# The fourth block of exponentials of each pair of heads is added by an adding DMA instead of by VectorE, in layer 0's attention

## The chip, the core and the metric

The kernel runs on one core of one Trainium2 chip. The metric is the device time of one execution in microseconds. Several runs are made of a kernel, and the median is given. One further execution is taken with the hardware profiler. The page and the trace describe that one execution, and its own time stands beside its span (the time from its first instruction to its last).

The engines are named as in the profile: PE is TensorE's matrix multiplication and PEld its loading of weights, DVE is VectorE, ACT is ScalarE, POOL is GpSimd, SP is SyncE, which here only issues DMAs. L1212 is line 1212 of the kernel.

## What is computed

The reference is a stack of four transformer-like layers on x of shape (4, 512, 128) in float32. Each layer is half a feed-forward block, an attention, and half a feed-forward block again. The change touches layer 0's attention alone:

```python
x = x + 0.5 * _L0_ffn_ref(_layernorm(x, axis=-1), ...)     # 8 experts, the 2 best of each token
x = x + _L0_attn_ref(_layernorm(x, axis=-1), ...)          # here
x = x + 0.5 * _L0_ffn_ref(_layernorm(x, axis=-1), ...)
...
# _L0_attn_ref: 16 heads of 64 channels, low-rank q, k and v, rotary positions on q and k
scores = jnp.einsum('bhqd,bhkd->bhqk', q, k) * scale       # 512 x 512 for each image and head
attn = jax.nn.softmax(scores, axis=-1)
out = jnp.einsum('bhqk,bhkd->bhqd', attn, v)
out = out.transpose(0, 2, 1, 3).reshape(b, s, H * DH)
out = out @ w_out.T + residual
```

There are 4 images (the first axis of x) of 512 tokens each. The softmax needs, for each image, head and query, the sum of 512 exponentials over the keys. How this sum is formed is what changes.

## The kernel before

**Layer 0's attention** is `l0_attn_quick` (L1191 to L1309). It works through 32 pairs of heads in order: 4 images, 8 pairs in each. P is 128, the number of partitions, S is 512, the number of tokens of an image, and NT is 4, the blocks of 128 keys.

For one pair, the scores are computed transposed, with keys on the partitions and queries along the row. For each block t of 128 keys, `score` (L1199) multiplies the block's keys with all 512 queries, for both heads, into one `big` tile of PSUM, 128 x 1024 (L1203). ScalarE takes the exponential of it into `pT` (L1204). A `pT` tile holds two blocks, so it is 128 x 2 heads x 2 blocks x 512 queries, and a pair fills two of them, one for each half. The pool has three `pT` buffers (`bufs=3`, in the loop) and three `big` ones (L282).

Then `value` (L1214) multiplies the four blocks with V, adding up in PSUM (L1217), and `add_up` (L1206) adds the four blocks of exponentials elementwise, into the pair's slice of the tile `sums`. It adds the first two blocks to each other (L1209) and then the third and the fourth to the sum (L1212, twice). The sum over the 128 partitions is left for later. A tile `sums` has 8 slices of 512, so it serves 4 pairs, and an image uses two of them; the pool has two. A slice of `sums` that a pair writes lies in one piece of 1024 elements in each partition.

Each pair also prepares later pairs. `l0_project` (L1149) multiplies out q and k of the pair after the next (L1153), ScalarE copies them out of PSUM (L1155), and two DMAs from SP's queue swap even and odd partitions into `other` (L1158). `l0_turned` (L1161) then rotates q and k of the next pair with three operations of VectorE, L1164 twice and L1165.

**The end of an image** (`end`, L1219) runs during the first pairs of the next image. Sixteen matrix multiplications L1223 add `sums` over the partitions, picking each head's row, in the order k outer and c inner; the second tile of `sums` is read in the second eight, and a pair's two slices are those of one c. VectorE takes the reciprocal (L1229, into `rsum`), TensorE spreads it over the channels (L1237, into `big` tiles), VectorE scales U with it (L1239), and TensorE multiplies with the output weights (L1246), which VectorE adds to x (L353). For the last image there is no next pair, so these steps stand alone.

**Other work runs in between**, in small steps from generators. One is the layer norm of the next image (`l0_begin`, L1168, with L318 to L331, L1172 on GpSimd and hT L1176). One is the routing of tokens to experts for the second feed-forward block (`route`, L499 to L596): its scatters L586 are indirect DMAs from GpSimd, 8 for each image. One is the gathering of rows from the first feed-forward block (`back`, L831, L842 on GpSimd and L837 on VectorE). GpSimd also sets `comb` to zero (L551) and takes a power in each layer norm (L322).

**The order of the work.** In this stage TensorE's instructions stand in the order of the program (`manual_schedule` with PE alone). The order on the other engines is made when the program is built, by a scheduler with estimates of durations, so taking an instruction away or putting one in can move others. Each engine's queue runs strictly in its order. Semaphores are put in by the framework: a buffer is written again only when every reader of its last content is done. For the rest of the program, after this attention, the order is made by a planner in the kernel (`run`, with `clock`), whose costs do not depend on this stage.

Of the kernel before, what the change touches and what calls it, by code (L numbers as in the profile page):

```python
# [13 lines left out]
ALU = mybir.AluOpType  # L14
# [256 lines left out]
def program(ctx: ExitStack, tc: tile.TileContext, a: dict, out: bass.AP, worst):  # L271

    nc = tc.nc
# [917 lines left out]
    def l0_attn_quick(w, work, head, made, first, early, late):  # L1191
# [14 lines left out]
        def add_up(half, s, pT):  # L1206

            if half == 0:
                nc.vector.tensor_tensor(s, pT[:, :, 0, :], pT[:, :, 1, :], ALU.add)  # L1209
            else:  # L1210
                for m in range(2):
                    nc.vector.tensor_tensor(s, s, pT[:, :, m, :], ALU.add)  # L1212

        def value(t, po, V, pT):  # L1214
            for u in range(2):
# [50 lines left out]
        for n, (b, hp) in enumerate(todo):  # L1266
# [23 lines left out]
            for half in range(2):  # L1290
                for t in (2 * half, 2 * half + 1):
                    value(t, po, made[b][1], pTs[half])
                add_up(half, sums[hp // 4][:, 2 * (hp % 4) : 2 * (hp % 4) + 2, :], pTs[half])
# [1534 lines left out]
```

## Time and profile before

| what | value |
|---|---|
| median of 3 runs (lowest to highest) | 1305.28 us (1298.9 to 1309.57) |
| the profiled execution, its time | 1288.94 us |
| the profiled execution, its span | 1287.2 us |
| mean granted clock of TensorE, of full speed | 0.965 |
| layer 0's attention, from the first exponential to the last sum over partitions | about 212 to 550 us |
| L1212 in the stage: number, mean, busy | 64, 1220 ns, 78.1 us |
| L1209 in the stage: number, mean, busy | 32, 1221 ns, 39.1 us |

The table of the profile's page has one row for each engine: busy time, its share of the span, and how many instructions it ran. "Busy" for PE does not mean that it works at its best rate, since the ends of its instructions are modelled. In a timeline a row has the start in us, the duration in us, the engine, the line, the operation, the tile written and the tiles read, their shapes, and how many instructions were merged into the row. In square brackets stands how long the engine had been idle before it and what ended that. In a list of waits a row has the waiting engine with its tile and line, the engine waited for with its own, and then the total in us, how often, and the longest.

### The profile page before, as it was taken

To read this page: it belongs to the slowest core of one execution; us is meant where nothing else is said; L and a number is where in the kernel's file an instruction comes from. 1 tells how busy PE (TensorE), PEld (TensorE's weight loads), DVE (VectorE), ACT (ScalarE), POOL (GpSimd) and SP (SyncE) were. 2 spreads that over 40 slices of the span, in tenths; PEclk is the share of its full clock that TensorE was granted. 3 is DMA by queue.
4 is the path that set the end of the run, shared out by engine and by line. 5 is a ranking of instruction groups with operands and counts; after the bars stand their busy time and mean duration, and the time that the engine had idled before them with its cause. 6 is when DMAs were issued, how large, how long until landed. Compare 5 with 4: busy or idle time off the path is not lost.

```text
span 1287.2 us, 20162 instructions
## 1 busy us (share of the span) xinstructions
PE 1174.3 (91%) x6954; PEld 630.3 (49%) x6954; DVE 895.4 (70%) x2328; ACT 700.6 (54%) x1015; POOL 328.1 (25%) x320
## 2 busy tenths in 40 slices
PE   5899989999999999988899949989999999999995
PEld 3455644334335335355455548765596544543333
DVE  5597767888988988769667945868735873365233
ACT  2435535653644544533345523556757777787872
POOL 4340223032220400202123554533224121041000
PEclk9899989999999999989899987899999999999998
DMA  8123311121110210201321140000011000000000
GB/s 308 33 73 90 89 60 52 66 76 38 57 66 33 80 48 37 67 1 40 106 73 44 36 133 23 26 12 23 26 50 38 5 18 18 17 25 1 9 9 11
DMA packets 63490, 65.00 MB, mean 50 GB/s; under 512 B 11538, under 2 KB 53908, under 8 KB 62868
## 3 DMA queue, kind: packets, MB, share of 16 engines
q1 hardware_dynamic: 57236, 51.04, 11.9%
q0 software_dynamic: 6144, 12.60, 3.3%
q8 instruction: 58, 0.95, 0.3%
q14 instruction: 52, 0.42, 0.1%
HBM read 29.13 MB, written 17.69 MB: 36 GB/s over the span
## 4 chain that ended last, share of the span: by engine, by line
PE 63%; DVE 21%; issue 5%; DMA 3%; ACT 3%; POOL 2%; SPq 1%; DVEq 0%; POOLq 0%; ACTq 0%
PE big L1956 8%; PE one L1998 8%; PE big L1203 5%; PE one L1217 5%; PE big L761 4%; PE one L1541 3%; PE big L883 3%; PE one L1246 2%; PE big L606 2%; DVE sums L1212 2%; PE big L1153 2%; PE one L2475 1%; PE one L2019 1%; PE big L635 1%; PE one L794 1%
## 5 line engine op out<-in xcount | busy, mean ns | idle before, releaser
L1972 ACT ACTIVATE pT<-big 128x1024 f32<-128x1024 f32 (+1 forms) x224 | 205.0, 963 | 52.7 <-PE big L1956 44.3
L1204 ACT ACTIVATE pT<-big 128x1024 f32<-128x1024 f32 x128 | 125.7, 1034 | 55.7 <-PE big L1203 53.0
L1203 PE MATMUL big<-qk 64*128 64x512 f32 x512 | 127.5, 609 | 6.8 <-DVE U L1239 6.8
L1956 PE MATMUL big<-qkq,qkk 32*128 32x512 f32 (+3 forms) x1024 | 130.9, 555 | 0.1
L1217 PE MATMUL one<-pT,V 128*64 128x512 f32 x512 | 116.9, 598 | 0.0
L1998 PE MATMUL one<-pT,V 128*32 128x512 f32 (+3 forms) x1024 | 111.5, 522 | 2.5 <-DVE through L2029 0.8
L1504 POOL TENSOR_TENSOR rs<-rs,root 128x4 f32<-128x4 f32 x35 | 37.1, 1059 | 226.8 <-DVE rs L1502 183.5
L586 POOL DMA_INDIRECT sorted_x<-xn,irows x64 | 70.9, 1108 | 69.8 <-DVE share L558 22.4
L1212 DVE TENSOR_TENSOR sums<-sums,pT 128x1024 f32<-128x1024 f32 x64 | 78.1, 1220 | 5.7 <-ACT pT L1204 1.1
L1203 PEld LDWEIGHTS big<-qk 64*128 64x128 f32 x512 | 46.6, 187 | 69.5 <-issue 40.9
L1956 PEld LDWEIGHTS big<-qkq,qkk 32*128 32x128 f32 x1024 | 49.2, 184 | 61.8 <-issue 40.8
L883 PE MATMUL big<-w_w,xsT 128*128 x156 | 76.2, 620 | 2.5 <-ACT xsT L1355 2.4
L761 PE MATMUL big<-w_w,xsT 128*128 x156 | 73.5, 595 | 0.4 <-issue 0.4
L1217 PEld LDWEIGHTS one<-pT,V 128*64 128x64 f32 x512 | 33.9, 136 | 77.1 <-issue 72.4
L842 POOL DMA_INDIRECT yg<-sorted_y,ito x32 | 40.1, 1254 | 123.0 <-DMA sorted_y<-ys 61.8
L1294 ACT COPY U<-one 128x512 f32<-128x512 f32 x32 | 18.8, 587 | 94.7 <-PE one L1217 92.6
L606 PE MATMUL big<-xnT,w_w 128*128 128x512 f32 x128 | 61.4, 616 | 6.9 <-DVE u L611 5.8
L353 DVE TENSOR_TENSOR x<-x,one 128x512 f32<-128x512 f32 x31 | 21.2, 684 | 57.2 <-PE one L1541 33.1
L1984 DVE TENSOR_TENSOR pT<-pT,w_c_tri 128x256 f32<-128x256 f32 (+1 forms) x96 | 52.4, 563 | 2.5 <-ACT pT L1972 2.2
L608 ACT ACTIVATE t<-big,w_bs 128x512 f32<-128x512 f32 x32 | 21.7, 685 | 56.5 <-PE big L606 30.9
L322 POOL TENSOR_TENSOR rs<-rs,root 128x4 f32<-128x4 f32 x16 | 20.7, 1298 | 118.7 <-DVE rs L321 118.6
L1998 PEld LDWEIGHTS one<-pT,V 128*32 128x32 f32 x1024 | 23.9, 108 | 54.6 <-issue 37.9
(448 smaller groups left out, 2418.4 us busy)
## 6 DMA issues: line engine op xcount, KB each, us to landing
other<-qk SPq DMA_DIRECT2D x64, 256.0 KB, 2.2
xs<-sorted_x SPq DMA_DIRECT2D x78, 64.0 KB, 1.8
sorted_y<-ys SPq DMA_DIRECT2D x38, 128.0 KB, 1.8
w_w<-in_w SPq DMA_DIRECT2D x2, 2048.0 KB
w_l_w<-in_l_w SPq DMA_DIRECT2D x8, 256.0 KB, 3.2
w_l_w<-in_l_w SPq DMA_DIRECT2D x1, 2048.0 KB, 8.4
X<-row_x SPq DMA_DIRECT2D x8, 256.0 KB, 3.5
row_y<-y SPq DMA_DIRECT2D x8, 256.0 KB, 2.3
```

Source lines behind the costliest of these rows:

```text
L586: apart(nc.gpsimd.indirect_dma_start(out=sorted_x[:, :], out_offset=bass.IndirectOffsetOnAxis(ap=irows[:, b, j, t : t + 1], axis=0), in_=x ...
L606: nc.tensor.matmul(pa[:, m, :], lhsT=w["w13"][:, NE, m, odd, c * P : (c + 1) * P], rhs=xTs[b], start=True, stop=True)
L761: nc.tensor.matmul(pa[:, k, :], lhsT=st[u]["xT"][:, k * P : (k + 1) * P], rhs=w["w13"][:, bass.ds(st[u]["e"][k], 1), m].rearrange("p o a b ...
L883: nc.tensor.matmul(pa[:, k, :], lhsT=xT[:, k * P : (k + 1) * P], rhs=w["w13"][:, bass.ds(e[k], 1), m].rearrange("p o a b -> p (o a b)"), s ...
L1203: nc.tensor.matmul(sT[:, u, :], lhsT=k[r, t * P : (t + 1) * P], rhs=q[r, :], start=True, stop=True)
L1204: nc.scalar.activation(pT[:, :, t % 2, :], sT, AF.Exp, scale=scale)
L1212: nc.vector.tensor_tensor(s, s, pT[:, :, m, :], ALU.add)
L1217: nc.tensor.matmul(po[r, :], lhsT=V[:, t, :], rhs=pT[:, u, t % 2, :], start=(t == 0), stop=(t == NT - 1), tile_position=(0, 64 * u))
L1956: nc.tensor.matmul(sT[j // 2][:, j % 2, c : c + n], lhsT=keys[k][r, t * P : (t + 1) * P], rhs=turns[k, g][r, S - n :], start=True, stop=True)
L1972: nc.scalar.activation(p[:, :, :n], sets[i][h][:, :, :n], AF.Exp, scale=scale)
L1984: nc.vector.tensor_tensor(d, d, w["c_tri"].unsqueeze(1).unsqueeze(1).to_broadcast([P, 2, len(parts), P]), ALU.min)
L1998: nc.tensor.matmul(po[32 * j : 32 * j + 32, S - n :], lhsT=V[k % 2][:, t, NJ * g + j, :], rhs=us[i][j // 2][:, j % 2, c : c + n], start=(t ...
```

## The change

In `add_up`, the third block is still added by VectorE (L1212). The fourth is no longer: a DMA issued from GpSimd reads the fourth block out of `pT`, and adds it to the slice of `sums` while it writes. It moves 128 partitions x 2 heads x 512 numbers, so 512 KB, for each of the 32 pairs. The DMA waits for the addition before it and for the fourth exponential; the sum over the partitions and the next writer of that `pT` buffer wait for the DMA.

```diff
@@ -1208,8 +1208,8 @@
             if half == 0:
                 nc.vector.tensor_tensor(s, pT[:, :, 0, :], pT[:, :, 1, :], ALU.add)
             else:
-                for m in range(2):
-                    nc.vector.tensor_tensor(s, s, pT[:, :, m, :], ALU.add)
+                nc.vector.tensor_tensor(s, s, pT[:, :, 0, :], ALU.add)
+                nc.gpsimd.dma_start(out=s, in_=pT[:, :, 1, :], accum_op=ALU.add)
 
         def value(t, po, V, pT):
             for u in range(2):
```

## The prediction

> **What bounds the kernel now.** I read first the page's busy times and its chain, then the busy time of the stage that the change lies in, then who makes TensorE wait there, then single timelines. The whole run:
>
> ```profile
> span 1287.2 us, 20162 instructions
> PE 1174.3 (91%) x6954; PEld 630.3 (49%) x6954; DVE 895.4 (70%) x2328; ACT 700.6 (54%) x1015; POOL 328.1 (25%) x320
> ```
>
> The 32 pairs of heads run from 212 to 550 us. The busy times of that stretch, and of two steady pairs in it (columns: stretch, length, then busy us and count of PE, PEld, DVE, ACT, POOL, the granted clock, the DMA share, GB/s):
>
> ```profile
> 212.00:550.00 338.00, 323.59 (x1622) 132.60 (x1620) 292.13 (x430) 174.42 (x204) 64.02 (x52) 0.99 0.15 56
> 223.00:239.20 16.20, 16.20 (x74) 5.81 (x72) 13.77 (x12) 10.61 (x13) 0.00 (x0) 1.00 0.16 65
> ```
>
> The reader is to see that TensorE is the bound: a pair takes 16.2/2 = 8.1 us and TensorE is busy in all of it, at a full clock, while VectorE is busy 13.77/2 = 6.9 us of the 8.1. In the whole stage TensorE idles only 338.0 - 323.6 = 14.4 us. Work taken from VectorE can give back no more than the part of these 14.4 us that VectorE causes. The waits of TensorE in the stage (us in total, times, longest):
>
> ```profile
> PE big L1203 <- DVE U L1239: 6.8, 6, 1.1
> PE big L1237 <- DVE rsum L1229: 5.0, 4, 1.9
> PE one L1179 <- DVE hT L1176: 1.3, 3, 0.6
> ```
>
> All three are VectorE's: 13.1 us, 1% of the span, the ceiling of any gain. Twelve of the 13.1 us lie in the four ends of an image (L1219 to L1251).
>
> **What is removed.** One of the 64 additions L1212 in each pair, so 32 x 1.22 us = 39 us of VectorE's 292 us. In steady pairs this is hidden wholly behind TensorE's 8.1 us. It is worth something where VectorE's order of work holds TensorE back. At the second image's end (VectorE's timeline):
>
> ```profile
> 378.73 1.23 DVE L1212 TENSOR_TENSOR sums<-sums,pT 128x1024 f32<-128x1024 f32 x1
> 379.87 3.35 DVE L1229 RECIPROCAL rsum<-one 128x512 f32<-128x512 f32 x1
> 383.14 1.16 DVE L1212 TENSOR_TENSOR sums<-sums,pT 128x1024 f32<-128x1024 f32 x1
> 384.22 1.21 DVE L1164 TENSOR_TENSOR qk<-qk,w_c_rope 128x1024 f32<-128x1024 f32 x1
> 385.35 1.22 DVE L1239 TENSOR_TENSOR U<-U,big 128x1024 f32<-128x1024 f32 x1
> ```
>
> The L1212 at 383.14 is one that goes. Both scalings of U behind it come 1.14 us earlier (the pitch of such additions in the chain of waits, 1.13 to 1.16), and TensorE waits 1.14 us before each of the two score blocks that need the banks U frees. The first wait vanishes and the second stays as long as it is, since TensorE arrives earlier too: 1.14 us won. The other two inner ends have the same order, L1212 at 292.34 and 471.72, so 3 x 1.14 = 3.4 us. The wait for rsum falls by another 1.14 us at the second end only (VectorE is busy without a gap before it; before the other two reciprocals it waits 2.7 and 3.5 us for TensorE itself). The hT waits hang on a chain VectorE-GpSimd-VectorE; I take half of their 1.3 us, 0.6. The last end has no L1212 behind its reciprocal. Gross gain 3.4 + 0.6 = 4.0 us, plus 1.1 us at the second end if nothing else delays it.
>
> **What is added: a transfer, and when it must have landed.** One adding DMA per pair, 128 partitions x 2 runs of 2 KB, 512 KB, on GpSimd's queue; it waits for the addition before it and for the fourth exponential. No adding DMA is in the trace. The nearest rows are the indirect DMAs on the same queue (min, median, max us from issue to landing) and the plain ones beside them:
>
> ```profile
> DMA to landing us min/median/max: 2.2/2.3/5.5
> q1 hardware_dynamic: 6672, 16.36, 12.3%
> other<-qk SPq DMA_DIRECT2D x60, 256.0 KB, 2.2
> ```
>
> The first is L586's, 64 KB in 128 rows. The second gives the rate: 16.36 MB in 12.3% of 338 us = 41.6 us, so 393 GB/s. From L586's 2.3 us: 448 KB more at that rate is +1.2 us; the sum must be read besides, 512 KB, +1.3; 256 runs instead of 128 rows to write descriptors for, +1.0 (an L586 keeps GpSimd 0.98 us). Estimate 5.8 us. Lower end: no second read and no longer issue, 2.3 + 1.2 = 3.5. Upper end: the slowest landing, 5.5, the longest issue seen (3.15 us, an L842) twice, and 3.3 us for the two and a half transfers: 15 us. I take 5.8, by the median row.
>
> The Trainium skill prices it otherwise: DMA: Bandwidth & Descriptors, "Anatomy of one DMA — SWDGE (gpsimd) path", has 2.0 us plus the bytes at 436 GB/s, 3.2 us here; Collectives: The Full Stack, "The bandwidth ceiling: the fold count and why AG ≠ RS ≠ AR", says that an add halves the rate since it reads two sources, so 2.0 + 2.4 = 4.4 us. No run here shows either yet. The sum is the same by 4.4 and by 5.8, because of the deadlines:
>
> First deadline: the block of exponentials. There are three pT buffers and a pair takes two, so the fourth block is overwritten by the first exponential two pairs on. Addition and exponential for one pair:
>
> ```profile
> 233.28 2.56 DVE L1212 TENSOR_TENSOR sums<-sums,pT 128x1024 f32<-128x1024 f32 x2
> ...
> 245.95 1.02 ACT L1204 ACTIVATE pT<-big 128x1024 f32<-128x1024 f32 x1 [0.47 <-PE big L1203]
> ```
>
> The first of the two additions ends at 234.5, the buffer is wanted at 245.95: 11.4 us. So taken for all pairs it is 9.7 us (the pair at 524.75) to 13 us, and 14 to 26 around the ends. 5.8 us fits with 4 us to spare. If that cover is gone, ScalarE's queue stops at that exponential, all later ones behind it; TensorE then runs out of `big` banks. Cost: half of each us over, per pair (the loop spans two pairs).
>
> Second deadline: the pick matmuls L1223 at the end of an image read the last pair's slice in the 12th of 16 steps. At the inner ends the addition is over 8.5, 5.2 and 9.1 us before that step: covered, but for 0.6 us at most at the second, which goes into the half-and-half below. At the last end nothing lies between: addition over at 540.2, landing 546.0, step wanted at 542.8 + 2.5 = 545.3: +0.7 us on the path, all of it, since reciprocal, spreading and output follow.
>
> Contention: 32 x 512 KB raise the DMA share from 0.15 by some 0.2; the `other` copies lie up to 2.7 us longer under it, but their consumer is the next pair's rotation, about 5 us or more away in steady pairs. Nothing. SP's queue is not touched otherwise.
>
> **What is added: work in GpSimd's queue.** 32 issues of about 2 us, in order with everything else there. Behind a waiting issue stand L322 and L1172 (layer norm for the next image, on which VectorE and hT hang), the gathers L842 and scatters L586, and a memset of `comb` (L551) that VectorE's L554 waits for. GpSimd is busy 64 of 338 us, so mostly it costs nothing. One place has no room:
>
> ```profile
> 364.29 0.99 POOL L842 DMA_INDIRECT yg<-sorted_y,ito  x1 [0.30 <-issue]
> 365.27 0.23 POOL L551 MEMSET comb<- 128x128 f32 x1
> 365.57 0.06 DVE L554 MEMSET comb<- 128x4 f32 x1 [4.58 <-POOL comb L551]
> ```
>
> Eleven indirect DMAs run from 349.25 without a gap, and VectorE loses 4.58 us to them. Two adding DMAs (additions over at 350.7 and 359.0) fall into this run: 2 x (2.0 + 0.3) = 4.6 us more, for the rotation behind L554 that TensorE needs within 0.8 us. VectorE makes good two additions on the way, 2.3 us: about +2.3 us (+2.9 with the 0.6) at this end instead of -1.1. At the third image the wait is 1.13 us and VectorE has 3.5 us idle before its reciprocal: covered. The order on VectorE, ScalarE and GpSimd is made at build time and may place the memset elsewhere; half and half, (2.9 - 1.1)/2 = +0.9.
>
> How long an issue is: the trace has 0.97 to 3.15 us for an indirect one, the longest (272.45) beside two-input additions of VectorE, which hold VectorE busy 86% of the stage. The Trainium skill, SBUF — State Buffer, "Who interferes with whom", says that GpSimd and VectorE share a port pair, that descriptor generation starves under VectorE's two-port copies and scalar operations, and that two-input operations hold back only GpSimd's reads. It speaks against this change only where such operations run, and here nearly all of VectorE's work has two inputs; this DMA reads no index. By the rule an issue stays near 2 us; by the row's worst it is 4 us, landing at 8, still under 9.7, and only the crowded place costs 4 us more. I take the rule's side.
>
> **The sum.** -3.4 - 0.6 + 0.9 + 0.7 = -2.4 us: span 1287.2 to 1284.8. The profiled execution took 1288.94 us (1.7 us lie outside the span); the median of the three runs is 1305.28, 1.3% above it. I carry the difference over unscaled: 1305.3 - 2.4 = 1303.
>
> **Rivals.** A, the forecast: landing under about 10 us, gains and losses of a few us cancel. For it: the deadlines above. 1291 to 1318.
> B, the wait moves to the buffer (slower): the time from the addition to the landing exceeds 11.4 us. About 26 pairs have less than 14 us, each us over costs 26 x 0.5 = 13 us. It decides (1%) from about 12.4 us on; at 15 us it is 3.6 x 13 = 47 us: 1350. For it: an add in the transfer, which no row prices, and issues that took up to 3.15 us; against: 5.8 is half of it.
> C, GpSimd's order (slower): an adding DMA stands behind the eight scatters L586, or a layer norm step behind an adding DMA. A run of eight lasts 12 us; a DMA behind it lands 12 + 5.8 - 11.4 = 6 us late, three images: +18 us, 1321. For it: L586 waited 22.4 us for one result of VectorE, with nothing behind it now; against: scatters and pairs are written in turn, two by two.
> D, VectorE was the real pace-maker (faster): the chain of waits runs through VectorE from 326 to 390, so up to all 13.1 us go: 1292. Against: TensorE was busy 59.5 of the 60 us from 320 to 380.
> E, the addition is only moved and nothing changes, 1305: part of A.
>
> **Numbers.** A (with E) 0.60, B 0.17, C 0.17, D 0.06. About 1%, 13 us, is what a measurement of this kernel can tell from no change. Slower by over 1%: B and C, 0.34; faster: D, 0.06; same 0.60. The range runs from 1291 (D's end) to 1350 (B at its upper bound); A's own range is 1291 to 1318.
>
> **What would show it.** Right: L1212 x32; per pair 8.1 us; no wait of pT L1204 for a DMA; U's waits on three fewer places; landing near 6 us. Wrong: ACT pT L1204 waiting for a DMA sums (B); VectorE waiting longer for comb or rs, or DMAs landing late because issued late (C). A landing over 11 us would make the prediction wrong by itself.

## The result, and the profile after

| | before | changed |
|---|---|---|
| median of 6 runs each on one chip | 1302.55 us (1291.24 to 1309.57) | 1313.23 us (1312.62 to 1319.67) |
| ratio, 95% interval | | 1.0129 (1.0098 to 1.0161) |
| profiled execution: time, span, granted clock | 1288.94, 1287.2 us, 0.965 | 1319.61, 1317.8 us, 0.957 |

By the ratio of the table the change costs 1.3%, 16.8 us (12.8 to 21.0). The two medians lie only 10.7 us apart, and the six runs of before spread over 18 us, so the size of the loss is known to a few us only. In the changed kernel L1211 is the third block's addition on VectorE and L1212 the adding DMA. Its page has, in the rows of busy time and of groups:

```profile
span 1317.8 us, 20215 instructions
PE 1186.9 (90%) x6954; PEld 635.3 (48%) x6954; DVE 860.5 (65%) x2296; ACT 700.9 (53%) x1015; POOL 362.6 (28%) x352
...
L1212 POOL DMA_DIRECT2D sums<-pT x32 | 40.0, 1285 | 136.7 <-ACT pT L1204 75.5
```

VectorE has 32 instructions and 35 us of busy time less, and the 32 issues take GpSimd 1.3 us each. The same two stretches as before, with the same columns (the first holds less of the stage than it did, since the stage is longer):

```profile
212.00:550.00 338.00, 320.40 (x1573) 132.19 (x1573) 252.90 (x400) 170.74 (x202) 96.25 (x83) 0.98 0.39 100
223.00:239.20 16.20, 16.20 (x74) 5.81 (x72) 11.89 (x10) 10.65 (x13) 2.58 (x2) 1.00 0.51 129
```

A steady pair still takes 8.1 us and TensorE fills it, so the loss lies at single places. The waits in the stage (us in total, times, longest):

```profile
ACT pT L1204 <- DMA sums<-pT: 16.4, 3, 6.4
DVE comb L554 <- POOL comb L551: 14.3, 2, 8.4
PE big L1153 <- ACT pT L1204: 8.5, 3, 4.5
PE big L1203 <- DVE U L1239: 6.8, 6, 1.1
PE big L1203 <- ACT pT L1204: 5.2, 1, 5.2
PE big L1237 <- DVE rsum L1229: 4.0, 4, 1.9
```

The first row is new: three times ScalarE's exponential waits for a buffer that an adding DMA is still reading. TensorE then waits for the exponential (third and fifth row). The first of the three places, as a timeline:

```profile
349.93 2.45 POOL L586 DMA_INDIRECT sorted_x<-xn,irows  x1 [2.37 <-issue]
351.34 1.22 DVE L1211 TENSOR_TENSOR sums<-sums,pT 128x1024 f32<-128x1024 f32 x1
...
361.70 0.98 POOL L586 DMA_INDIRECT sorted_x<-xn,irows  x1 [0.30 <-issue]
362.99 1.07 POOL L842 DMA_INDIRECT yg<-sorted_y,ito  x1 [0.30 <-issue]
364.05 1.37 POOL L1212 DMA_DIRECT2D sums<-pT  x1
...
369.17 2.85 ACT L1204 ACTIVATE pT<-big 128x1024 f32<-128x1024 f32 x3 [5.69 <-DMA sums<-pT]
369.76 0.06 DVE L554 MEMSET comb<- 128x4 f32 x1 [8.36 <-POOL comb L551]
370.25 2.08 PE L1153 MATMUL big<-cT,w_up_qk 64*128 64x512 f32 x4 [4.53 <-ACT pT L1204]
```

The addition that the DMA follows is over at 352.56. The DMA is issued at 364.05, since GpSimd has to get through the run of eight scatters L586 and a gather first. It lands 5.1 us later, at 369.17, and only then does the exponential run for which ScalarE has been free since 363.48. The other two places are alike: the DMA is issued behind the eight scatters, at 457.67 and 549.08, and ScalarE is released at 462.77 and 554.15 after 4.38 and 6.36 us. TensorE idles 4.53 + 3.22 + 5.20 = 12.95 us at the three.

From the first exponential to the start of L1223 at the last end, the traces have 328.9 us before and 344.5 after, 15.6 more. The intervals between the ends grow by 5.1, 3.4 and 7.4 us. Of TensorE's waits 12.95 us are new and 2.3 are gone (1.0 of rsum, 1.3 of hT). Its busy time grew by 5.1 us (321.0 to 326.2), with a granted clock of 0.98 instead of 0.99.

In part this clock varies from one profiled execution to the next: experiment 1, without these waits, shows it in one image (87.4 us busy at 0.98, against 85.0 at 1.00). But it is not chance alone. In experiment 2, which keeps the three waits, TensorE is busy for 327.8 us at 0.97, and the mean clock of its six runs is 0.9640, against 0.9705 for the 35 runs of before beside it. In experiments 1 and 3, without the waits, it is busy for 322.4 and 322.7 us, at mean clocks of 0.9672 and 0.9706. Among those 35 runs, 0.01 of clock goes with 7.9 us of time, so about 5 us of the loss (an estimate) come with a lower clock and not with the waits themselves. Whether the waits lower the clock was not separated.

The six waits for U have not changed at all. VectorE at the first end:

```profile
293.26 3.35 DVE L1229 RECIPROCAL rsum<-one 128x512 f32<-128x512 f32 x1
296.53 1.16 DVE L1164 TENSOR_TENSOR qk<-qk,w_c_rope 128x1024 f32<-128x1024 f32 x1
297.61 1.21 DVE L1164 TENSOR_TENSOR other<-other,w_c_rope 128x1024 f32<-128x1024 f32 x1
298.74 1.21 DVE L1239 TENSOR_TENSOR U<-U,big 128x1024 f32<-128x1024 f32 x1
```

Where the addition stood, the scheduler has put the second L1164. U is scaled as late as before.

### The profile page after: what moved, and what is told of

Same layout as the page of the kernel before. It is cut to its first block, busy times and chain, and to the rows that moved or that the text cites. A ratio compares the mean times of both kernels' runs of the same rounds, so it can differ in the third digit from the quotient of the medians.

```text
span 1317.8 us, 20215 instructions
## 1 busy us (share of the span) xinstructions
PE 1186.9 (90%) x6954; PEld 635.3 (48%) x6954; DVE 860.5 (65%) x2296; ACT 700.9 (53%) x1015; POOL 362.6 (28%) x352
## 3 DMA queue, kind: packets, MB, share of 16 engines
q0 software_dynamic: 14848, 29.37, 10.2%
## 4 chain that ended last, share of the span: by engine, by line
PE 36%; DVE 11%; DMA 3%; issue 2%; POOL 2%; ACT 2%; SPq 1%; POOLq 0%; DVEq 0%; ACTq 0%
PE big L1956 8%; PE one L1998 7%; PE one L1541 3%; PE big L883 2%; PE one L2475 1%; PE big L606 1%; PE one L2019 1%; PE one L2456 1%; PE one L2393 1%; PE big L2393 1%; DVE us L903 1%; DVE pT L1984 1%; PE one L1246 1%; DMA yg<-sorted_y,ito 1%; PE one L1531 1%
## 5 line engine op out<-in xcount | busy, mean ns | idle before, releaser
L1204 ACT ACTIVATE pT<-big 128x1024 f32<-128x1024 f32 x128 | 125.8, 1033 | 70.9 <-PE big L1203 54.0
L1504 POOL TENSOR_TENSOR rs<-rs,root 128x4 f32<-128x4 f32 x35 | 37.1, 1059 | 236.9 <-DVE rs L1502 194.0
L586 POOL DMA_INDIRECT sorted_x<-xn,irows x64 | 74.2, 1159 | 52.1 <-issue 23.2
L1212 POOL DMA_DIRECT2D sums<-pT x32 | 40.0, 1285 | 136.7 <-ACT pT L1204 75.5
L842 POOL DMA_INDIRECT yg<-sorted_y,ito x32 | 34.5, 1078 | 116.5 <-DMA sorted_y<-ys 62.2
L1209 DVE TENSOR_TENSOR sums<-pT 128x1024 f32<-128x1024 f32 x32 | 39.0, 1219 | 30.7 <-ACT pT L1204 17.2
L1164 DVE TENSOR_TENSOR qk<-qk,w_c_rope 128x1024 f32<-128x1024 f32 x32 | 38.9, 1216 | 27.2 <-DMA other<-qk 24.2
```

Of the source, the lines that this page charges most:

```text
L586: apart(nc.gpsimd.indirect_dma_start(out=sorted_x[:, :], out_offset=bass.IndirectOffsetOnAxis(ap=irows[:, b, j, t : t + 1], axis=0), in_=x ...
L1204: nc.scalar.activation(pT[:, :, t % 2, :], sT, AF.Exp, scale=scale)
L1212: nc.gpsimd.dma_start(out=s, in_=pT[:, :, 1, :], accum_op=ALU.add)
```

## The experiments

The theory after this trace: the loss comes from the place in GpSimd's queue. Three adding DMAs stand behind eight scatters, so the pT buffer comes free late. Rivals: VectorE held up by the late memset of comb (14.3 us); the adding transfers themselves, too long or in the way; GpSimd's 32 issues. Each kernel's ratio is to the kernel before on the same chip, with a 95% interval.

**1. The order alone.** GpSimd's instructions of the stage in the order of the program.

```diff
-        with tc.manual_schedule(engines={mybir.EngineType.PE}):
+        with tc.manual_schedule(engines={mybir.EngineType.PE, mybir.EngineType.Pool}):
```

> The changed kernel, with GpSimd's instructions of this stage in the order of the program, so that at most four scatters L586 stand ahead of an adding DMA instead of eight. Nothing else is added or taken away. Theory (the adding DMA is queued behind eight scatters, so the pT buffer comes free 3 to 6 us late at three places): the three waits of pT L1204 for the DMA that writes sums (16.4 us in all in the changed kernel) shrink under 3 us in all, the three inner ends give back 13 to 16 us, and the time is 0.997 to 1.002 of before. Rival 1 (the late memset of comb holds VectorE for 8.4 us and that is what costs): the memset moves too, so this run alone does not part it from the theory; the waits of pT L1204 do. Rival 2 (32 adding DMAs are too long or crowd the DMA engines, wherever they are issued): the waits stay and the time stays at 1.010 to 1.016 of before. Rival 3 (GpSimd's 32 issues cost by themselves): stays at 1.010 to 1.016 too.

Measured: 1.0028 (1.0011 to 1.0045). All 32 DMAs remain, and in the list of waits none is left of pT L1204 for a DMA. TensorE's:

```profile
PE big L1203 <- DVE U L1239: 6.8, 6, 1.1
PE big L1237 <- DVE rsum L1229: 3.2, 3, 1.8
PE one L1223 <- DMA sums<-pT: 2.8, 2, 1.5
```

Four fifths of the loss go with the order. This speaks against rivals 2 and 3 (the transfers themselves, and their issues). The third row is new: with TensorE no longer late, the last sums of two images land 1.5 and 1.3 us after it wants them. The time came out 0.1% above the range that I gave.

**2. The memset.** VectorE zeroes comb itself; the scatters stay ahead.

```diff
-            nc.gpsimd.memset(comb, 0.0)
+            (nc.vector if slow else nc.gpsimd).memset(comb, 0.0)
```

> The changed kernel, with the tile comb zeroed by VectorE instead of GpSimd in the routing of the first three images. The scatters stay ahead of the adding DMAs. Theory (late pT buffer): the waits of pT L1204 for the DMA that writes sums stay near 16 us in all, and the time stays at 1.010 to 1.016 of before, although VectorE no longer waits for comb. Rival 1 (VectorE held by the late memset): the 14.3 us of waiting for comb are gone, TensorE's idle time at the three ends goes with them, and the time is 0.997 to 1.003 of before. Rivals 2 and 3 (the adding DMA itself, or its issues): no change, as in the theory.

Measured: 1.0149 (1.0108 to 1.019). The wait for comb of 8.4 us is gone, that of 6.0 us at the third image is not, so the edit took away 8.4 of the 14.3 us. The waits for the buffer stay:

```profile
ACT pT L1204 <- DMA sums<-pT: 18.2, 3, 7.1
```

At the place of the timeline above:

```profile
355.69 0.17 DVE L551 MEMSET comb<- 128x128 f32 x1 [1.47 <-PE one L568]
355.93 0.06 DVE L554 MEMSET comb<- 128x4 f32 x1
358.18 1.37 POOL L1212 DMA_DIRECT2D sums<-pT  x1
362.25 1.34 POOL L1212 DMA_DIRECT2D sums<-pT  x1
363.28 2.86 ACT L1204 ACTIVATE pT<-big 128x1024 f32<-128x1024 f32 x3 [7.14 <-DMA sums<-pT]
364.36 2.08 PE L1153 MATMUL big<-cT,w_up_qk 64*128 64x512 f32 x4 [5.99 <-ACT pT L1204]
```

VectorE no longer waits for GpSimd there, and TensorE waits longer than in the changed kernel (5.99 against 4.53 us). Rival 1 falls at this place.

**3. Three pairs undone.** Only the pairs whose DMA stood behind the scatters get VectorE's addition back.

```diff
-                nc.gpsimd.dma_start(out=s, in_=pT[:, :, 1, :], accum_op=ALU.add)
+                nc.vector.tensor_tensor(s, s, pT[:, :, 1, :], ALU.add) if back else nc.gpsimd.dma_start(out=s, in_=pT[:, :, 1, :], accum_op=ALU.add)
...
-                add_up(half, sums[hp // 4][:, 2 * (hp % 4) : 2 * (hp % 4) + 2, :], pTs[half])
+                add_up(half, sums[hp // 4][:, 2 * (hp % 4) : 2 * (hp % 4) + 2, :], pTs[half], b > 0 and hp == 5)
```

> The changed kernel, but the fourth block is added by VectorE again for 3 of the 32 pairs: the sixth pair of images 1, 2 and 3, those whose adding DMA stood behind the eight scatters. 29 adding DMAs stay. Theory (three late DMAs make all of the loss): the waits of pT L1204 for a DMA nearly vanish and the time is 0.997 to 1.003 of before; where the order of GpSimd then puts another pair's DMA behind the scatters, it waits again and gives back only part. Rival 2 (length and crowding of all 32 transfers) and rival 3 (their issues): 29 of 32 stay, so the time is still 1.009 to 1.015 of before.

Measured: 1.0022 (1.0 to 1.0045). Of the three waits, a single one of 1.1 us remains. The wait for comb has stayed:

```profile
DVE comb L554 <- POOL comb L551: 10.4, 2, 7.0
```

The longer of the two, 6.95 us, lies at the first of the three places, and TensorE loses 0.50 us there, waiting for the rotation behind it. So rival 1 falls as a whole: the late memset is nearly free where the buffer is not late. On the same chip experiment 2, with all 32 DMAs in the poor order (and the memset moved), is at 1.0149. So three of 32 transfers make (1.0149 - 1.0022) x 1283.6 = 16 us, the lower clock that comes with them included, and the other 29 make some 3 us (0 to 6).

**4. The price of the add.** A plain DMA in the same place.

```diff
-                nc.gpsimd.dma_start(out=s, in_=pT[:, :, 1, :], accum_op=ALU.add)
+                nc.gpsimd.dma_start(out=s, in_=pT[:, :, 1, :])
```

> The changed kernel with a plain DMA of the same bytes from the same place in the queue: it overwrites the sum instead of adding to it, so the addition of the fourth block (and with it the other three) is left out of the result. It prices the add. If an add costs a second read of the destination, landing comes 1.3 to 1.5 us sooner than the 5.1 us measured, the queue's time for 512 KB falls from 2.9 to about 1.4 us, and each of the three waits of pT L1204 is shorter by as much: 12 us in all instead of 16.4. If the add costs nothing and the number of runs or the queue sets the length, all three stay. By the theory the waits stay in either case, since most of their length is the place in the queue.

One run, 1281.24 us beside a median of 1283.59; one run says nothing about 0.2%. The DMA view of the stage for an adding kernel in which GpSimd's queue has the same order but for the memset (experiment 2; queue, packets, MB, share of 16 engines over 385 us, then the median us from issue to landing):

```profile
q0 software_dynamic: 9888, 19.21, 25.9%
...
sums<-pT POOLq DMA_DIRECT2D x32, 512.0 KB, 4.9
```

and for the plain copy:

```profile
q0 software_dynamic: 5792, 19.21, 12.7%
...
sums<-pT POOLq DMA_DIRECT2D x32, 512.0 KB, 3.1
```

The add costs 1.8 us of landing (expected 1.3 to 1.5) and (25.9% - 12.7%) x 385 / 32 = 1.6 us of the DMA engines for each transfer. An issue takes GpSimd 0.75 us instead of 1.22. Though the plain copy stands behind the same eight scatters, the three waits fell from 16.4 to 8.5 us, more than I expected. A shorter landing accounts for 3 x 1.8 = 5.4 of the 7.9 us. For the rest, the traces show that the time from the addition to the issue was also shorter at two of the three places, by 0.9 and 1.4 us; in single traces that can be chance.

**5 and 6. The two orders without the DMA.** Experiment 5 is the kernel before with the edit of experiment 1. Experiment 6 is the kernel before with the first scaling of U put ahead of the next rotation (an import and the start of the list `ahead` are left out here):

```diff
-                        nc.vector.tensor_tensor(u, u, pr[:, :, :N], ALU.mult)
+                        i = nc.vector.tensor_tensor(u, u, pr[:, :, :N], ALU.mult).ins; ahead[:] = ahead if k else [i]
...
-                        qk[n + 1] = l0_turned(w, *raw[n + 1])
+                        with tc.issue_after(ahead.pop()) if ahead else nullcontext(): qk[n + 1] = l0_turned(w, *raw[n + 1])
```

> The kernel before (all additions on VectorE), with GpSimd's instructions of this stage in the order of the program. The control for the order by itself. Theory (the order matters only because a buffer's release stands behind the scatters): no adding DMA, so nothing is late; 0.998 to 1.002 of before. Rival (the order of the program is better for GpSimd anyhow, and the gain of the changed kernel in that order came from there): 0.987 to 0.992 of before.

> The kernel before, with the first scaling of U (L1239) at an inner end put ahead of the next pair's rotation L1164 in VectorE's order; the additions stay on VectorE. The prediction gave 3.4 us of gain to U's waits; the changed kernel did not show it, since a rotation L1164 moved into the place of the addition that was gone. Theory (VectorE's order there sets the waits, not its load): the six waits of big L1203 for U (6.8 us in all) vanish and nothing takes their place, 0.9935 to 0.997 of before. Rival (the rotation is then late itself and TensorE waits for qk instead): 0.998 to 1.003.

Measured: 0.9983 (0.9962 to 1.0004) and 0.9986 (0.9963 to 1.0009). The first is the theory's. The second lies between its two expectations: U's waits fell from 6.8 to 1.8 us, but 1.7 us came back at L1246, since the addition L1212 still stands ahead of U.

**7 and 8. The changed kernel with both orders,** and the same with VectorE's addition back at the two ends where the sums landed late (the edit of experiment 3 with `b in (1, 3) and hp == 7`).

> The changed kernel with both orders: GpSimd in the order of the program, and U's scaling ahead of the rotation. Theory: the sum of the two, 1.0028 for the first and -6.8 us for the second, so 0.996 to 0.999 of before, and 2 to 4 us slower than the kernel before with U first, since the last sums land late at two ends (1.3 and 1.5 us). Rival (the relief of VectorE is worth something once the orders are good): as fast as the kernel before with U first or faster, 0.993 to 0.996.

> As the run before this one (changed kernel, both orders), but for the last pair of the second and of the fourth image VectorE adds the fourth block again, so 30 adding DMAs. At these two ends TensorE waited 1.5 and 1.3 us for the sums to land. Theory (these waits are what is left of the loss): L1223 waits no more, 0.993 to 0.996 of before, level with the kernel before with U first within 2 us: the other 30 DMAs neither gain nor lose. Rival (DMAs in steady pairs cost something by themselves, such as slower transfers beside them): it stays 2 us or more above that kernel. Other rival (they gain): it is 2 us or more below it.

Measured: 0.9942 (0.9922 to 0.9961) and 0.9952 (0.9934 to 0.9969). Experiment 7 lies in its rival's range and not in the theory's. In experiment 8 L1223's waits did vanish, but the time did not fall below that of experiment 7, and at 4.4 us under experiment 6 it came out as its second rival (the DMAs gain) has it. So the offload now seemed to gain 5 us. But experiment 6 differs from both in the order of GpSimd too; hence the last four.

**9 to 12. Four kernels on one chip,** all with GpSimd in order: adding by VectorE or by DMA, with U behind the rotation or ahead of it.

> First of four kernels that are run on one chip, all with GpSimd in the order of the program: the fourth block added by VectorE or by the adding DMA, each with U's scaling behind the rotation (as the scheduler puts it) or ahead of it. Up to here such kernels were compared through the kernel before on different chips. This one: VectorE adds, U late (a kernel run before, again). 0.997 to 1.001 of before, whatever the theory.

> Second of the four (the changed kernel with GpSimd in order, again): adding DMA, U late. Theory (an addition taken from VectorE pays only if what follows it moves up, and here a rotation L1164 takes its place): level with the first of the four or up to 3 us slower (sums landing late at two ends), 0.998 to 1.003. Rival (the offload gains some 5 us whatever the order, as the last pair of kernels suggested): 0.993 to 0.997.

> Third of the four (new: the kernel before, GpSimd in order, U first): VectorE adds, U first. From the trace of the kernel before with U first, U's waits fall from 6.8 to 3.5 us (1.8 for the score blocks, 1.7 for the output): 3.3 us under the first of the four, 0.994 to 0.998.

> Fourth of the four (again): adding DMA, U first. Theory: the missing addition now does pay at the three inner ends, 1.8 + 1.7 - 0.7 = 2.8 us, and the late sums cost 3.6 us; so within 2 us of the third of the four, and 5 to 6 us under the second. Rival (the offload gains 5 us or more beyond the waits that the trace shows): 4 us or more under the third of the four, as 0.9942 against 0.9986 had it on another chip.

| ratio to before | U behind the rotation | U ahead of it |
|---|---|---|
| VectorE adds | 0.9991 (0.9975 to 1.0007) | 0.9959 (0.9941 to 0.9977) |
| adding DMA | 1.0023 (1.0003 to 1.0043) | 0.9959 (0.9942 to 0.9977) |

TensorE's waits with U ahead, VectorE adding:

```profile
PE big L1237 <- DVE rsum L1229: 4.0, 4, 1.9
PE one L1246 <- DVE U L1239: 1.9, 5, 0.4
PE big L1203 <- DVE U L1239: 1.8, 3, 0.6
```

and with the adding DMA:

```profile
PE big L1237 <- DVE rsum L1229: 3.2, 3, 1.9
PE one L1223 <- DMA sums<-pT: 2.9, 2, 1.5
PE big L1237 <- DVE U L1239: 1.0, 1, 1.0
...
PE big L1203 <- DVE U L1239: 0.8, 3, 0.3
```

With U behind the rotation the DMA loses 0.3%, about 4 us. Its trace has 3.5 us of waits for late sums, and no gain at U. But the mean clock of its 22 runs is also lower, 0.9644 against 0.9675, so how the 4 us divide is not settled. With U ahead the missing addition pays 1.8 + 1.9 - 0.8 = 2.9 us in the waits, and the late sums (2.9 us) take it away again. The third and the fourth kernel are level, as the theory has it; the fourth is 8 us under the second, where 5 to 6 were expected. The apparent 5 us of the offload is not confirmed: 0.4% under the kernel before is reached without the change.

One thing stays open. From the first exponential to the end of the last L1223, the four traces take 331.7, 337.7, 328.5 and 326.8 us, and experiment 8, where the two late ends are back on VectorE, takes 322.6, 5.9 less than the third kernel. These are single executions. In the times it cannot be seen: from there to its end the program, which no edit touches there, takes 730 to 752 us in the profiled executions of the twelve experiments. And experiment 8 and the third kernel did not run on one chip (0.9952 and 0.9959). That 30 adding DMAs gain something in the best order is neither shown nor excluded.

## Why the prediction failed

**The bound** was read rightly: a steady pair is TensorE's, 8.1 us before and after.

**The failed step is GpSimd's queue**: "GpSimd is busy 64 of 338 us, so mostly it costs nothing", and against rival C "scatters and pairs are written in turn, two by two". That is the order of the program, which binds TensorE alone in this stage. GpSimd's is made at build, and there the eight scatters stand together. The trace of before already showed it:

```profile
349.25 1.07 POOL L586 DMA_INDIRECT sorted_x<-xn,irows  x1 [2.80 <-DVE xa L331]
...
360.16 1.16 POOL L586 DMA_INDIRECT sorted_x<-xn,irows  x1 [0.30 <-issue]
361.63 1.05 POOL L842 DMA_INDIRECT yg<-sorted_y,ito  x1 [0.30 <-issue]
```

The prediction used this run for the memset of comb only, and took it that two adding DMAs would stand within it. Had it asked what happens if one stands behind, the first deadline had the answer. Rival C's own sum was good: 12 + 5.8 - 11.4 = 6 us of lateness at each of three places. At the first the trace shows 11.5 us from addition to issue, 5.1 to landing, and 10.9 from the addition until ScalarE was free: 5.7. C's 18 us stand against 16.4 of ScalarE's waiting, 12.95 of TensorE's and 16.8 measured. That the last is so near is partly luck: C took each us of lateness whole (rival B took the half of it), four fifths of it reached TensorE, and about 5 us came with the lower clock, which is in no sum. Its chance of 0.17 was the error. Experiments 1 and 3 show the cause: they part the three DMAs from the scatters in two different ways, and both times the waits and most of the loss go.

**U's 3.4 us** did not come. The step "Both scalings of U behind it come 1.14 us earlier" assumed that the rest of VectorE's order stays; a rotation L1164 took the place. The mechanism is seen in the waits: with U pinned ahead, the missing addition is worth 2.9 us.

**hT**: 0.6 expected, all 1.3 us gone. **rsum at the second end**: 1.66 to 0.70 us, near the 1.14 expected. It is not shown to be the missing addition's: in experiment 5, where VectorE still adds and only GpSimd's order was set otherwise, this wait is 0.71 us as well.

**The memset of comb**, +4.6 us of delay at half a chance: it did come late, VectorE's wait there growing from 4.58 to 8.36. Taking that wait away (experiment 2) bought nothing, so in the changed kernel its price is hidden behind the late buffer. By itself it costs little: in experiment 3 the wait is 6.95 us, 2.4 more than before, and TensorE loses 0.50 us by it.

**The landing**: 5.8 us from issue estimated, 4.9 measured in experiment 1 (4.8 to 6.2). The two estimates from the Trainium skill come closer. The rule of DMA: Bandwidth & Descriptors, "Anatomy of one DMA — SWDGE (gpsimd) path", gives 3.2 us without the add, and 3.1 were measured. With the halved rate of Collectives: The Full Stack, "The bandwidth ceiling: the fold count and why AG ≠ RS ≠ AR", which the page states for a ReduceScatter in a ring of cores and not for a single DMA, it is 4.4, and 4.9 were measured: the add costs 1.8 us and not 1.2. The terms that I added to the indirect DMA's 2.3 us made it too long, without effect on the sum. The first deadline held for all 32 pairs once the queue was right, so rival B was rightly kept low.

**The second deadline** was cut too fine: 0.6 us at most at the second end and 0.7 at the last. The changed kernel shows 0.5 at the last (the picks took 4.18 us instead of 3.64) and none at the second, where TensorE was late itself. Without that lateness (experiments 1, 3 and 7, and the second and fourth of the last four) TensorE waits 1.4 to 2.1 us at the second and 0.6 to 1.6 us at the last. **Contention** cost nothing, though not by the distance of 5 us that the prediction gave: VectorE's rotation does wait for `other`, 18.3 us in all instead of 2.9, but TensorE waits for no rotation. The copies themselves landed in 2.3 us (median, experiment 1) instead of 2.2. **Issues** of about 2 us took 1.22 (1.17 to 1.82).

## What to carry to other kernels

When an operation moves to another engine's queue, its deadline must be set against the longest unbroken run in that queue as it is built, not against the engine's mean load or the order of the source. A buffer with 11 us of slack is safe from a 5 us transfer and not from 11.5 us of queue ahead of it. An operation taken away from an engine whose order a scheduler makes pays only if what others wait for moves into its place. Here pinning U ahead of the rotation was worth 0.6% with the change and 0.3% without it, so that the change, which lost 0.3% before, came out level.

## What the hardware showed that I had not expected

An adding DMA is split finer than a plain one. Over the whole run GpSimd's queue has 14848 packets with the adding DMA and 10752 with the plain one, 4096 / 32 = 128 more for each transfer of 128 partitions. GpSimd's issue grows from 0.75 to 1.22 us with it.

The place in the queue matters for the neighbours too. Where the scatters L586 stand together ahead of the adding DMAs (experiments 2 and 3) they land in 2.3 us (median), as they do before the change and beside the plain copy. Where they stand between adding DMAs (experiment 1) they take 3.6 us. Whether plain copies between them would do the same was not tried.
